# Turning a quarter of the attention blocks on VectorE and the DMA queues: a graph attention layer followed by a top-p diffusion layer

## The chip, the cores and the metric

The kernel runs on one NeuronCore of a Trainium2 chip. The core has TensorE (PE; its weight loads are listed apart as PEld), VectorE (DVE), ScalarE (ACT), GpSimd (POOL) and SyncE (SP), which here only issues DMA transfers. The metric is the device time of one launch in microseconds (us), lower being better: a median over runs, beside one execution that the hardware profiler recorded.

## The reference

The inputs are `x` (4096 rows of 256 floats) and a 0/1 adjacency matrix `adj` (4096 x 4096). Layer 0 is a graph attention layer with four heads. Layer 1 normalizes its input and then makes two steps of a diffusion with two hops each, one over the graph and one over an attention matrix that keeps, row by row, the largest probabilities until their sum reaches 0.9. The change lies in the first of these two steps.

```python
def _top_p_attention(X, W1, W2, W3):
    q = X @ W1.T @ W2.T
    k = X @ W3.T
    probs = jax.nn.softmax(q @ k.T / TAU, axis=-1)
    idx = jnp.argsort(-probs, axis=-1)
    sp = jnp.take_along_axis(probs, idx, axis=-1)
    cs = jnp.cumsum(sp, axis=-1)
    keep_sorted = cs - sp < TOP_P
    ...
    A = probs * mask
    return A / jnp.maximum(A.sum(-1, keepdims=True), 1e-12)
...
for n in range(STEPS):              # STEPS = 2
    A = _top_p_attention(Xa, W1, W2, W3)
    Xf = R @ Xf
    Xa = A @ Xa
    Z = Z + Xf @ U1[n].T + Xa @ U2[n].T
```

## The kernel before

Rows are cut into 32 blocks (`NB`) of 128. Layer 0 and the first graph hop fill the first 1068 us or so of the span. Then comes step 0 of the top-p attention (n = 0), then step 1, which is built the same way, with the second graph hop at its start.

**One block.** For block b of 128 query rows the kernel makes 128 x 4096 logits (`logits`, L758; four calls of four matmul instructions, 512 columns each), takes their exponentials into the tile `e` on ScalarE (`exponentials`, L944), and sums them under two bounds, also on ScalarE (`first_probe`, L949, four passes over half a row). GpSimd works out a better bound `c3` from these sums in a chain of small operations (`first_step`, L968, ending at L1000). VectorE then copies everything below `c3` into the tile `big` (`third_probe`, L1015), searches `big` for the threshold (`candidates`, L1018 to L1053: 18 MAX8 passes at L1033, a reduction over 18 numbers that lie 8 floats apart at L1037, MAX8 and MATCH_REPLACE on the survivors, a scan and some small operations), and sets all smaller exponentials in `e` to zero (`masked`, L1055, the long instruction at L1058, then a reciprocal at L1059).

**The product.** `attend` (L1154) multiplies the masked row block by the 4096 x 256 matrix `X`. The matrix product wants the row block turned: its columns have to lie on the partitions. So for each of eight groups g of four column blocks, `turn` (L1121) makes four TensorE transposes of 128 x 128 squares into PSUM and one ScalarE copy of the four to SBUF (`eT`, L1126), and `gather` (L1129) makes four matmuls that add up in `acc`. Each fp32 matmul of `gather` runs as two weight loads and two passes, so a group has eight instructions at L1132. `turn` runs two groups ahead of `gather`. After the eighth group come `contributed` (L1140: four more instructions at L1142) and `scaled` (L1134: a ScalarE copy and a store to `xa_d`).

**What runs beside it.** While TensorE attends to block b, it also makes the logits of block b + 3 (`AHEAD`), a call of `logits` after each of the first two turns and after the first two gathers, and ScalarE makes their exponentials and probes. GpSimd's chain for block b + 3 follows when the probes are done. Blocks 0 to 2 are searched earlier, during the first graph hop (`picks`). The last three blocks (29 to 31) have no block ahead and make no logits.

**The order.** All of this is emitted under `manual_schedule`, so each engine runs its instructions in the order of the Python calls. For each b the loop at L1450 calls `chosen_kept(b)` (L1409), then `began` for block b + 3, then `attend(b)`. On VectorE the order in `chosen_kept(b)` is: the search of block b, `third_probe` of block b + 1, `finish` of block b - 2 (L1311), `masked` of block b. Block 31 has no `third_probe` behind it. On the SP queue the order around a block is: the store to `xa_d` of block b - 1 (it waits for the end of that block's product), the store to `z_d` of `finish`, two small loads of `q_s` for a later block (L770), the load of `xf` for block b (L1111), and then the store to `xa_d` of block b.

**Buffers.** `e` has four buffers. The pool `rp` has a tag `ar` with four buffers of 128 x 1024 floats, which hold adjacency tiles in the graph hops and lie unused while step 0 attends.

Of the kernel before, what the change touches and what calls it, by code (L numbers as in the profile page):

```python
# [11 lines left out]
F32 = mybir.dt.float32  # L12
# [14 lines left out]
P = 128  # L27
# [13 lines left out]
G0 = 8  # L41
# [15 lines left out]
def gat_then_top_p_diffusion(  # L57
# [18 lines left out]
    nc = tc.nc  # L76
# [4 lines left out]
    NB = N // P  # L81
# [6 lines left out]
    dram = ctx.enter_context(tc.tile_pool(name="dram", bufs=1, space=bass.MemoryType.DRAM))  # L88
# [33 lines left out]
    rp = ctx.enter_context(tc.tile_pool(name="rp", bufs=2))  # L122
# [35 lines left out]

    uv_d = dram.tile([H, P, NB, 2, W3 + 1], BF16, name="uv_d")
    s_d = dram.tile([H, N], F32, name="s_d")  # L160
    adj_d = dram.tile([NB // G0, P, NB, G0 * P], F32R, name="adj_d")
    with tc.tile_pool(name="l0", bufs=1) as l0, tc.tile_pool(name="l0s", bufs=2) as l0s, tc.tile_pool(name="l0o", bufs=1) as l0o:
        passing = ctx.enter_context(ExitStack())
# [410 lines left out]
        with tc.manual_schedule(engines=every):  # L574
# [14 lines left out]
            for k in range(KC):  # L589
                for c in range(KC):  # L590
                    nc.tensor.matmul(pm[:, k, :], w_t[:, k, c, :], spots[:, c].rearrange("p t h -> p (t h)"),
                                     start=(c == 0), stop=(c == KC - 1))
# [15 lines left out]
            for n, (k, p) in enumerate(todo):  # L608
# [16 lines left out]
                if k % H == 2 and 2 < p < PAIRS - 3 and lifted:  # L625
                    b = lifted.pop(0)
# [128 lines left out]
    def bank():  # L755
        return ps2.tile([P, 2, 512], F32, name="mm")[:, 0, :]

    def logits(q, kT, c):  # L758

        pm = ps2.tile([P, 2, 512], F32, name="mm")  # L760
        for t, halves in enumerate(((0, 1), (1, 0))):
            for h in halves:
                nc.tensor.matmul(pm[:, h, :], q[t], kT[:, ds(h * (N // 2) + c * 512, 512)], start=(t == 0), stop=(t == 1))  # L763
        return pm
# [143 lines left out]
    def col(name, bufs=None):  # L908
        return small.tile([P, 1], F32, name=name, bufs=bufs or 4)
# [34 lines left out]
    def exponentials(r, c):  # L944

        ev = r.e.rearrange("p (h c n) -> p h c n", h=2, c=4)
        nc.scalar.activation(ev[:, :, c, :], r.pm[c], AF.Exp, bias=r.nm, accum_out=r.sums[:, c // 2, c % 2:c % 2 + 1])  # L947
# [107 lines left out]
    def masked(r):  # L1055

        kept, r.scale = col("kept"), col("scale")
        nc.vector.scalar_tensor_tensor(r.e, r.e, r.t, r.e, ALU.is_ge, ALU.mult, accum_out=kept)  # L1058
        nc.vector.reciprocal(r.scale, kept)  # L1059
# [24 lines left out]
    def untied(r, z, work):  # L1084
# [18 lines left out]
        nc.vector.scalar_tensor_tensor(r.e, ties, r.t, r.e, ALU.mult, ALU.add, accum_out=kept)  # L1103
        nc.vector.reciprocal(r.scale, kept)

    def block(t, b):
        return t[ds(b, 1)].rearrange("o p d -> (o p) d")

# [12 lines left out]
    def turn(r, g):  # L1121
        pt = ps3.tile([P, 4, P], F32, name="tp")
        for i in range(4):
            nc.tensor.transpose(pt[:, i, :], r.e[:, ts(4 * g + i, P)], ident)  # L1124
        eT = rows.tile([P, 4, P], F32, name="eT", bufs=3)
        nc.scalar.copy(eT, pt)  # L1126
        return eT

    def gather(r, eT, g, cur):  # L1129
        for i in range(4):  # L1130
            j = 4 * g + i
            nc.tensor.matmul(r.acc[:, 0, :], eT[:, i, :], cur[:, j, :], start=(j == 0), stop=(j == NB - 1))  # L1132

    def scaled(r):  # L1134
        if r.n + 1 < STEPS:
# [4 lines left out]
    def contributed(r):  # L1140
        for k in range(KC):
            nc.tensor.matmul(r.far, r.xf[:, k, :], S.u1[:, k, :], start=(k == 0), stop=(k == KC - 1))  # L1142
# [11 lines left out]
    def attend(r, cur, ahead, between={}, eT=()):  # L1154

        if ahead:
            ahead.pm = {}
        def start(c):
            if ahead:
                ahead.pm[c] = logits(ahead.q, ahead.kT, c)  # L1160
                exponentials(ahead, c)
        eT = list(eT) or [turn(r, 0)]
        start(0)
        loads(r)
        r.ri = rinv[:, r.b:r.b + 1]
        last = r.n + 1 == STEPS and r.b + 1 == NB
        if last:
            r.far = bank()[:, :D]
        eT.append(turn(r, 1))
        start(1)  # L1170
        for g in range(NB // 4):
            if g + 2 < NB // 4:
                eT.append(turn(r, g + 2))
            gather(r, eT[g], g, cur)
            if last and g == 4:
                contributed(r)
                weighed(r)
                gathered(r)
            if g < 2:
                start(2 + g)  # L1180
            elif g == 2 and ahead:
                summed(ahead)
            elif g in PROBED and ahead:
                first_probe(ahead, PROBED.index(g))
            if g in between:
                between[g]()
        if not last:
            contributed(r)
            weighed(r)
        scaled(r)  # L1190
# [193 lines left out]
    for n in range(STEPS):  # L1384
        cur = X
        G = SimpleNamespace()
        found = [table(f"found{i}") for i in range(3)]
        blocks = {}
        with tc.manual_schedule(engines=every):
            pieces = first_hop if n == 0 else hops(second)  # L1390
            filling, picking = fills(n, G, found, blocks), picks(n, found, blocks)
            done = 0 if n else NB - G0 - LOOK
            for i, _ in enumerate(pieces, 2 * done):
                if n > 0 and i % 6 == 1 and i // 6 < NB // 4:
                    g = i // 6
                    nc.sync.dma_start(cur[:, ts(g, 4), :], xa_d[ts(g, 4)].rearrange("b p d -> p b d"))
                if (n == 0 or i > 10) and i // 2 % NB != NB - 2:
                    next(filling, None)
                    if i // 2 % NB < NB - 3 or i % (2 * NB) == 2 * NB - 1:
                        next(picking, None)  # L1400
                if i == 2 * len(order) - 6:
                    first = turn(blocks[0], 0)
            weights(n)
            for _ in filling:
                next(picking, None)
            for _ in picking:
                pass

            def chosen_kept(b):  # L1409

                r = blocks[b]
                if not hasattr(r, "kept"):
                    candidates(r, found)
                if b > 2:
                    polished(blocks.pop(b - 3))
                if b + 1 < NB and not hasattr(blocks[b + 1], "thirded"):
                    third_probe(blocks[b + 1])
                if b > 1:
                    finish(blocks[b - 2])
                    finish_scale(blocks[b - 2])  # L1420
                if b + 2 < NB and not hasattr(blocks[b + 2], "stepped"):
                    first_step(blocks[b + 2])
                if 0 < b < NB - 1:
                    gathered(blocks[b - 1])
                if not hasattr(r, "kept"):
                    masked(r)
                if 1 < b < NB - 1:
                    normal(blocks[b - 2])

            R = SimpleNamespace(n=n, kT=G.kT, qT=G.qT, nm=G.nm, table=found[0])  # L1430

            def last_chosen():
                chosen_kept(NB - 1)
                R.failed, R.undone = questioned(G, found)

            def looked():
                counted(R)
                chosen(R)

            def beginning():  # L1440
                normal(blocks[NB - 3])
                gathered(blocks[NB - 2])
                finish(blocks[NB - 2])
                finish_scale(blocks[NB - 2])

            def asked():
                R.count = number(R, R.undone)

            beside = {NB - 2: {5: last_chosen}, 0: dict(zip((0, 1, 3, 5, 6), S.turned))}
            for b in range(NB - 1):  # L1450
                chosen_kept(b)
                if b + AHEAD < NB:
                    blocks[b + AHEAD] = began(n, b + AHEAD, G)
                attend(blocks[b], cur, blocks.get(b + AHEAD),
                       beside.get(b, {}), [first] if b == 0 else ())
            r = blocks[NB - 1]

            def earlier():
                polished(blocks[NB - 3])
                finish_rows(blocks[NB - 2])  # L1460

            beside = {0: beginning, 1: looked, 3: earlier, 4: asked}
            if n + 1 < STEPS:
                second = hop_of(n + 1)
                beside.update({2: lambda: (both_weights(), begin(second, 5)), 5: lambda: split(second, 2), 6: lambda: (split(second, 5), own(second, 5))})
            attend(r, cur, None, beside)
            for m in range(second.begun if n + 1 < STEPS else 0):
                for s in range(KC):
                    graph_products(second, m, s, (0,))
            finish(r)  # L1470
            finish_scale(r)
            finish_rows(r)
        repaired(R, cur)
# [32 lines left out]
```

## Time and profile before

| What | us |
|---|---|
| Median of three runs | 2820.71 (2817.5 to 2821.74) |
| The profiled execution | 2820.09 |
| Its span, first to last instruction | 2818.1 |
| Step 0, first turn to the last product's store | 1068.4 to 1768.4 |
| One block of step 0 (1404.34 to 1426.27, store to store) | 21.93 |
| TensorE's mean granted clock, as a share of full speed | 0.996 |

The profile's page gives the busy time of each engine over the span, the same in 40 equal slices (about 70 us each), the DMA queues, and the costliest groups of instructions, each with a count, a mean duration and the idle time of its engine in front of it with what ended that idle time. Other views give busy time in chosen windows, the list of waits, and instructions in order of time. Durations of neighbours on an engine overlap a little: the next instruction of VectorE can start some 0.07 us before the one in front of it is said to end, so that a sequence is best read from start to start.

### The profile page before, as it was taken

The page shows a single profiled execution, that of the slowest core. Times are in us where ns is not written, and L with a number is a line of the kernel's source. Part 1 is how long each engine was busy: PE and PEld are TensorE (multiplying, and loading weights), DVE is VectorE, ACT ScalarE, POOL GpSimd, SP SyncE. Part 2 cuts the span into 40 slices and gives each one's busy share as a digit, 9 for nine tenths or more (in the row PEclk, how much of TensorE's full clock was granted, in tenths as well). Part 3 has the DMA queues.
Part 4 walks back from the last instruction along what each step waited for, and adds up shares of the span by engine and source line. Part 5 has one row for each costly group of instructions (what it writes and reads, how often), then busy time and mean ns, then how long its engine had stood idle before and what let it go on. Part 6 is the DMA issues. An engine that isn't in the chain of part 4 may idle for free. (4 is left out here: it accounts for less than half of the span.)

```text
span 2818.1 us, 51577 instructions
## 1 busy us (share of the span) xinstructions
PE 2772.0 (98%) x18791; PEld 2443.1 (87%) x18791; DVE 2164.6 (77%) x5067; ACT 1925.4 (68%) x3066; POOL 907.2 (32%) x1895
## 2 busy tenths in 40 slices
PE   6999999999999999999999999999999999999998
PEld 5899999999988888888888888667878888888887
DVE  8877878778654385999989997333574999999997
ACT  8867886879633636888888884232627878887882
POOL 7311121111011231223332231000304666666664
PEclk9999999999999999999999999999999999999999
DMA  9969597695376782000000002667991111111110
GB/s 204 255 247 197 210 233 196 228 203 217 143 229 213 242 305 94 21 21 21 27 20 21 21 24 69 217 196 239 332 348 50 32 34 40 31 32 32 37 34 26
DMA packets 174114, 376.44 MB, mean 134 GB/s; under 512 B 18198, under 2 KB 123542, under 8 KB 169750
## 3 DMA queue, kind: packets, MB, share of 16 engines
q1 hardware_dynamic: 142496, 271.12, 29.9%
q0 software_dynamic: 26112, 97.53, 13.8%
q10 hardware_dynamic: 5238, 4.35, 0.5%
q8 instruction: 153, 2.51, 0.4%
q14 instruction: 115, 0.94, 0.1%
HBM read 305.48 MB, written 113.57 MB: 149 GB/s over the span
## 5 line engine op out<-in xcount | busy, mean ns | idle before, releaser
L1132 PE MATMUL acc<-X,eT 128*128 128x256 f32 x4096 | 948.0, 379 | 0.0
L1132 PEld LDWEIGHTS acc<-X,eT 128*128 128x128 f32 x4096 | 748.1, 190 | 85.7
L400 PE MATMUL acc<-ut,m 128*128 128x195 bf16 (+1 forms) x8192 | 698.1, 246 | 1.2 <-DVE m L379 0.9
L400 PEld LDWEIGHTS <-m 128*128 128x128 fp8e4 x8192 | 696.8, 97 | 2.4 <-DVE m L379 1.5
L372 ACT ACTIVATE g<-sr,d_big 128x1024 uint8<-128x1024 f32 x448 | 473.0, 1135 | 9.9 <-DVE m L378 9.9
L947 ACT ACTIVATE e<-mm,nm 128x1024 f32<-128x1024 f32 x256 | 286.4, 1119 | 178.3 <-PE mm L763 167.4
L1126 ACT COPY eT<-tp 128x512 f32<-128x512 f32 x512 | 297.0, 581 | 80.1 <-PE tp L1124 79.8
L1033 DVE MAX8 cand<-big 128x8 f32<-128x228 f32 (+1 forms) x1152 | 348.3, 380 | 0.0
L646 PE MATMUL mm<-ar,hl 128*128 128x512 f32 x848 | 336.4, 407 | 3.8 <-DMA ar<-adj_d 1.7
L1015 DVE SCALAR_TENSOR_TENSOR big<-e,c 128x4096 f32<-128x4096 f32 x58 | 261.4, 4506 | 87.0 <-POOL c L1000 56.9
L646 PE MATMUL acc<-ar,hl 128*128 128x512 f32 x848 | 324.1, 393 | 1.3 <-DVE ar L490 1.3
L1124 PE MATMUL tp<-ident,e 128*128 128x128 f32 x2048 | 306.4, 273 | 5.3 <-ACT eT L1126 3.1
L1124 PEld LDWEIGHTS tp<-ident,e 128*128 128x128 f32 x2048 | 254.2, 141 | 65.7 <-ACT eT L1126 4.5
L378 DVE TENSOR_TENSOR m<-g,ax 128x512 uint32<-128x512 uint32 x256 | 188.7, 737 | 97.4 <-PE acc L400 76.9
L1058 DVE SCALAR_TENSOR_TENSOR e<-e,found 128x4096 f32<-128x4096 f32 x58 | 259.0, 4466 | 0.0
L954 ACT ACTIVATE void<-e,c 128x2048 int8<-128x2048 f32 x128 | 257.0, 2008 | 0.9
L954 ACT ACTIVATE void<-e,c1x 128x2048 int8<-128x2048 f32 x128 | 256.9, 2007 | 0.9
L971 POOL TENSOR_TENSOR sums<-sums 128x2 f32<-128x2 f32 x64 | 12.7, 199 | 623.7 <-ACT void L954 622.2
L379 DVE TENSOR_TENSOR m<-m,ax 128x512 uint32<-128x512 uint32 x256 | 183.2, 715 | 25.7 <-PE acc L400 0.5
L646 PEld LDWEIGHTS mm<-ar,hl 128*128 128x128 f32 x848 | 159.6, 188 | 43.7 <-issue 9.5
L763 PE MATMUL mm<-kT,qT 128*128 128x512 f32 x512 | 192.4, 457 | 1.5 <-ACT e L947 1.5
L646 PEld LDWEIGHTS acc<-ar,hl 128*128 128x128 f32 x848 | 159.3, 188 | 37.7 <-issue 4.1
(311 smaller groups left out, 3525.6 us busy)
## 6 DMA issues: line engine op xcount, KB each, us to landing
ar<-adj_d SPq DMA_DIRECT2D x212, 512.0 KB, 4.7
adj_d<-ax POOLq DMA_DIRECT2D x32, 2048.0 KB, 7.7
ut<-uv_d SPq DMA_DIRECT2D x60, 784.0 KB, 6.4
aru<-adj_d SPq DMA_DIRECT2D x44, 512.0 KB, 4.5
ax<-in_adj_t_dram POOLq DMA_DIRECT2D x32, 512.0 KB, 18.3
x<-xf_d SPq DMA_DIRECT2D x78, 128.0 KB, 5.2
xf<-xft_d SPq DMA_DIRECT2D x64, 128.0 KB, 2.3
sr<-s_d SPq DMA_DIRECT2D x15, 512.0 KB, 4.9
```

Source lines behind the costliest of these rows:

```text
L372: nc.scalar.activation(g[:, c, :], shared[k].sr, AF.Relu, scale=BIG, bias=d_big[:, h, j:j + 1])
L400: nc.tensor.matmul(shared[k].acc[i][:, t, :cols], m[t][:, c, ts(i, P)], shared[k].ut[j // QUARTER][:, j % QUARTER, t, :cols], start=(j == ...
L646: nc.tensor.matmul(A.acc[c][s], A.hl[m][:, t, ts(s, P)], A.ar[m][:, ts(c, 512)], start=(j == 0 and t == 0), stop=(j == NB - 1 and t == 1))
L763: nc.tensor.matmul(pm[:, h, :], q[t], kT[:, ds(h * (N // 2) + c * 512, 512)], start=(t == 0), stop=(t == 1))
L947: nc.scalar.activation(ev[:, :, c, :], r.pm[c], AF.Exp, bias=r.nm, accum_out=r.sums[:, c // 2, c % 2:c % 2 + 1])
L954: nc.scalar.activation(void, r.e[:, ts(h, N // 2)], (AF.Relu, AF.Sign)[i], bias=r.c1, scale=-1.0, accum_out=r.sums[:, h, 2 + i:3 + i])
L1015: nc.vector.scalar_tensor_tensor(big, r.e, r.c3, r.e, ALU.is_le, ALU.mult, accum_out=r.low3)
L1033: nc.vector.max(cand[:, s, :], big[:, edges[s]:edges[s + 1]])
L1058: nc.vector.scalar_tensor_tensor(r.e, r.e, r.t, r.e, ALU.is_ge, ALU.mult, accum_out=kept)
L1124: nc.tensor.transpose(pt[:, i, :], r.e[:, ts(4 * g + i, P)], ident)
L1126: nc.scalar.copy(eT, pt)
L1132: nc.tensor.matmul(r.acc[:, 0, :], eT[:, i, :], cur[:, j, :], start=(j == 0), stop=(j == NB - 1))
```

## The change

For blocks 3 to 30 of step 0 the last quarter of the row block, the eight column blocks 24 to 31 (`SENT` = 24), is no longer turned by TensorE. Directly behind `masked(r)` the new function `sent(r)` is called. One VectorE instruction transposes 32 x 32 squares inside the 1024 last columns of `e` and writes them to a tile `staged`, arranged so that the eight column blocks are interleaved: neighbours in a row of a square land 8 floats apart. A square that has been turned in place lies on the wrong group of 32 partitions, so DMA moves it: four stores of 128 KB each put the squares into a DRAM tensor `turned_d` (one store for each group of 32 columns, in runs of 1 KB), and one load of 512 KB, which has to wait for the four, brings them back to a tile `landed` with each square on its right partitions, 4 KB for each partition. All five DMAs are issued from SP. In `attend`, groups 6 and 7 are not turned (no transposes, no `eT` copy), and their eight matmuls in `gather` take their weights from `landed`, where the 128 floats of one partition lie 8 floats apart. Both tiles use the `ar` buffers, two for each block. Blocks 0 to 2 and 31 of step 0 and all of step 1 are left as they were.

```diff
+    turned_d = dram.tile([NB, 4, 32, 4, 2 * P], F32, name="turned_d")
...
+    SENT = NB - 8
+
+    def sent(r):
+        wide, many = (NB - SENT) * 32, NB - SENT
+        stage = rp.tile([P, G0 * P], F32, name="staged", tag="ar", bufs=4)
+        nc.vector.transpose(stage[:, :4 * wide].rearrange("p (c s b) -> p c b s", c=4, b=many),
+                            r.e[:, ds(SENT * P, many * P)].rearrange("p (b c r) -> p c b r", b=many, c=4))
+        landed = rp.tile([P, G0 * P], F32, name="landed", tag="ar", bufs=4)
+        for c in range(4):
+            nc.sync.dma_start(turned_d[r.b, c].rearrange("r q x -> q r x"), stage[:, ts(c, wide)])
+        nc.sync.dma_start(landed[:, :4 * wide], turned_d[r.b].rearrange("c r q x -> (c r) (q x)"))
+        r.landed = landed[:, :4 * wide].rearrange("p (i b) -> p b i", b=many)
...
     def gather(r, eT, g, cur):
...
-            nc.tensor.matmul(r.acc[:, 0, :], eT[:, i, :], cur[:, j, :], start=(j == 0), stop=(j == NB - 1))
+            nc.tensor.matmul(r.acc[:, 0, :], r.landed[:, j - SENT] if eT is None else eT[:, i, :], cur[:, j, :], start=(j == 0), stop=(j == NB - 1))
...
     def attend(r, cur, ahead, between={}, eT=()):
...
-                eT.append(turn(r, g + 2))
+                eT.append(None if hasattr(r, "landed") and 4 * (g + 2) >= SENT else turn(r, g + 2))
...
     def chosen_kept(b):
...
                 if not hasattr(r, "kept"):
                     masked(r)
+                    if b < NB - 1 and r.n == 0:
+                        sent(r)
```

## The prediction

> **What bounds the kernel now.** First the page's busy times, its slices and the granted clock:
>
> ```profile
> PE 2772.0 (98%) x18791; PEld 2443.1 (87%) x18791; DVE 2164.6 (77%) x5067; ACT 1925.4 (68%) x3066; POOL 907.2 (32%) x1895
> ...
> PE   6999999999999999999999999999999999999998
> ...
> DVE  8877878778654385999989997333574999999997
> ...
> PEclk9999999999999999999999999999999999999999
> ```
>
> TensorE is busy nearly throughout at full clock. Step 0 (1068 to 1768 us) covers slices 16 to 25, where VectorE shows nines as well. So the stage has to be read for itself, in the view of busy time by windows (PE, PEld, DVE, ACT, POOL):
>
> ```profile
> 1400.00:1500.00 100.00, 100.00 (x529) 86.85 (x528) 89.72 (x239) 81.27 (x131) 35.06 (x110) 1.00 0.08 24
> ```
>
> In 100 us of step 0 TensorE has no gap, VectorE is busy 89.7 us and ScalarE 81.3. The list of waits between 1200 and 1600 us says what VectorE's rest is:
>
> ```profile
> DVE big L1015 <- POOL c L1000: 27.2, 18, 1.5
> ```
>
> Once in each of 18 blocks, 1.51 us on average, `third_probe` waits for GpSimd's `c3`. Beside the small gaps between its instructions that is all the time VectorE has off. Then the timeline of one block:
>
> ```profile
> 1412.01 4.48 DVE L1015 SCALAR_TENSOR_TENSOR big<-e,c 128x4096 f32<-128x4096 f32 x1 [1.51 <-POOL c L1000]
> ...
> 1414.75 0.60 PE L1124 MATMUL tp<-ident,e 128*128 128x128 f32 x4
> ...
> 1415.19 1.89 PE L1132 MATMUL acc<-X,eT 128*128 128x256 f32 x8
> ...
> 1416.81 4.47 DVE L1058 SCALAR_TENSOR_TENSOR e<-e,found 128x4096 f32<-128x4096 f32 x1
> 1416.92 0.60 PE L1124 MATMUL tp<-ident,e 128*128 128x128 f32 x4
> ...
> 1419.52 5.34 PE L1132 MATMUL acc<-X,eT 128*128 128x256 f32 x24
> ...
> 1421.21 0.08 DVE L1058 DVE_READ_ACCUMULATOR e<-e,found 128x1 f32 x1
> ...
> 1424.70 1.03 PE L1142 MATMUL acc<-u,xf 128*128 128x256 f32 x4
> ...
> 1425.35 0.58 PEld L1124 LDWEIGHTS tp<-ident,e 128*128 128x128 f32 x4
> ```
>
> Three things are to be seen. **A group** (four transposes, eight passes) lasts 1416.92 - 1414.75 = 2.17 us; 24 passes alone last 1424.70 - 1419.52 = 5.18 us, 0.216 each; so four transposes cost 2.17 - 8 x 0.216 = 0.44 us. **VectorE's lead**: `masked` ends at 1421.29 and TensorE first needs it at 1425.35, 4.1 us later. **The periods**: `third_probe` starts at 1149.06, 1170.98 and 1192.89, a block each 21.92 us, TensorE's pace. VectorE without its wait would need 21.92 - 1.51 = 20.41.
>
> **The change part by part.** *Removed from TensorE:* eight transposes for each of 28 blocks, 2 x 0.44 = 0.89 us a block. TensorE alone would run at 21.03, and the most that can be won is 28 x 0.89 = 24.9 us. *Removed from ScalarE:* two copies of 0.58 us; with 19% of its time free it bounds nothing, so this counts as nothing (were that idle time gone, it would be a gain of up to 1.16 us a block).
>
> *Added to VectorE:* one transpose of 128 x 1024 floats a block, behind `masked`. Nothing waits for it at once (TensorE's first turn waits for `masked` only), but the search of the next block is queued behind it, and behind that the next `masked`. VectorE's period becomes 20.41 + T, where T is counted from start to start. With T over 0.62 VectorE is slower than TensorE's 21.03 and its lead runs out; with T over 1.51 it is slower than today. No row shows this instruction. Its floor is a comparison of 1024 elements (L370) that took 720 ns at the shortest, T = 0.65. At one element a cycle, the slope of the reductions below (1.06 ns), with 0.14 us fixed and 0.07 off for the overlap, T = 1.16. Its ceiling is the slowest kind of row per element: the scan (L1045) took 326 ns for 48 elements beside 196 ns for one element (L1036), 2.8 ns each, T = 2.9. Between them stands what the instruction does that most of VectorE's rows don't: it writes neighbours 8 floats apart. One row reads at just this step, the reduction over the eighth of each eight candidates; beside it stand a reduction over 512 neighbours and one over 32 at a step of 2:
>
> ```profile
> L829 DVE TENSOR_REDUCE lengths<-xs x16: 685/686/689, 830.7 to 1914.5; 128x8 f32<-128x512 f32 x16
> ```
> ```profile
> L847 DVE TENSOR_REDUCE km<-lengths x2: 178/178/178, 903.3 to 1924.4; 128x1 f32<-128x32 f32 x2
> ```
> ```profile
> L1037 DVE TENSOR_REDUCE found<-cand x64: 174/184/191, 996.0 to 2777.1; 128x1 f32<-128x18 f32 x64
> ```
>
> The first two give (686 - 178) / 480 = 1.06 ns an element and 144 fixed, so 18 elements should take 163 ns. They took 184 (174 to 191): 1.17 ns more for each (0.6 to 1.6). At 1.06 + 1.17 = 2.23 ns, T = 1024 x 2.23 + 0.14 - 0.07 = 2.35 us; with the shortest and longest of that row, 1.79 and 2.74. I take 2.35, since this row shares engine and step; that it reads where the transpose writes, and that 21 ns are small, is why both ends are kept.
>
> [...]
>
> *The stage's end.* Blocks 29 to 31 have no logits and TensorE needs only 18.64 us for each (1710.44, 1729.08, 1747.78), so today's lead has shrunk to 1.0 at block 30 (`masked` ends at 1728.12). From `masked` of block 3 to that of block 30 are 27 periods; the change of the end is 27 x (20.41 + T - 21.92) less this 1.0, and less some 0.5 that block 30's product still saves: **27 x (T - 1.51) - 1.5**. With T = 2.35 that is 22.7 - 1.5 = +21.2 us.
>
> *Moved to PE's weight loads:* 16 loads a block from `landed`, whose floats lie 8 apart. Rows of such a load are missing; the nearest and the longest of its size:
>
> ```profile
> L1132 PEld LDWEIGHTS acc<-X,eT 128*128 128x128 f32 x4096 | 748.1, 190 | 85.7
> ...
> L591 PEld LDWEIGHTS b<-spots,w_t 128*128 128x128 f32 x8 | 1.8, 332 | 0.0
> ```
>
> A load of 190 ns hides under a pass of 216. Up to 216 the new ones cost nothing; at 332 (the longest row, at the kernel's start) each adds 0.116, 1.86 us a block, and TensorE's period is 22.89. Up to 323 they lie under VectorE's 22.76. I take nothing, because VectorE's period covers them, and keep 332 for the range: 28 x (22.89 - 21.92) = +27. [...]
>
> *Added to SP:* four stores and a load a block, behind the store to `xa_d` of the block before and ahead of the two `q_s` loads and `xf`. An issue takes up to 0.55 us (1.10 for two `q_s`).
>
> ```profile
> q_s<-qT SPq DMA_DIRECT2D x128, 32.0 KB, 1.9
> xa_d<-xa SPq DMA_DIRECT2D x32, 128.0 KB, 1.7
> ...
> X<-xa_d SPq DMA_DIRECT2D x8, 512.0 KB, 5.2
> ```
>
> Counted from `masked`: 2.35 for the squares, 4 x 0.55 to issue, 1.8 to land, 0.55 to issue the load, which waits for the four, 5.2 to land (the 512 KB row): 12.1 us. The first pass of group 6 starts 17.6 us into a block today (1403.64 to 1421.25) and 16.7 with two turns gone, so 4.6 us are spare. `q_s` serves a later block, and `xf` is needed 20 us in, so their delay of some 5 us is hidden too. DRAM and the 7% DMA share (the page's slices show 20 to 27 GB/s here) leave room for 1 MB a block.
>
> *The sum:* 2820.09 (the profiled execution, of which 2818.1 is span; 0.6 under the median of the runs) + 21.2 = **2841 us**.
>
> **The rivals.** *The transpose runs at an element a cycle.* For it: the tensor reductions and arithmetic all do; against it: the 184 ns row. T = 1.16 gives 27 x (-0.35) - 1.5 = -11: 2809 us, **faster**. It decides for T under 1.57, and clears 0.2% under 1.36. At 0.65 TensorE bounds again, at up to -24.9: 2795.
>
> *Weight loads bound.* For it: 16 loads with no adjacent floats; against it: 133 ns of room over today's load. From 323 ns on it takes VectorE's place; at 332 2847; were the loads slowed as much as that reduction's elements (2.23 / 1.06, 400 ns), TensorE's period would be 21.03 + 16 x 0.184 = 23.97 and the time 2820 + 28 x 2.05 = 2877.
>
> *The load lands too late.* It would show at group 6, and decide from 4.6 + 1.7 us of lateness on (1.7 being VectorE's excess over TensorE); with the slowest 512 KB row of the page, 18.3 us for `ax`, the load would come at 25.2, 8.5 late, and the time grow by 28 x (21.03 + 8.5 - 21.92) = 213 us. Against it: that row belongs to layer 0 under heavy traffic.
>
> *A T near the break-even*, 1.36 to 1.78: within 5.6 us of today.
>
> **How the numbers follow.** VectorE's write bounds, T from 1.79 to 2.74: 0.52, its own range 2826 to 2852. Weight loads: 0.14. Late landing: 0.04. An element a cycle or faster: 0.19. Near the break-even: 0.11. Two tenths of a percent, 5.6 us, is what a measurement can tell from no change: faster 0.19, same 0.11, slower 0.70. The range takes in half of the element-a-cycle case, 2809, and reaches on the other side into the weight loads, 2857.
>
> **What would show it.** A VectorE row of 28 transposes near 2.4 us; no more wait of `third_probe` for GpSimd; instead TensorE idle once a block, some 1.7 us, at the first turn, waiting for `masked`; a period of 22.8 us. Loads from `landed` above 216 ns with passes spaced wider in the last 16 of a block would show the second rival, a wait on `landed` at group 6 the third. A transpose near 1.2 us would make the forecast wrong.

## The result, and the profile after

The changed kernel takes **2832.64 us** (median of six runs, 2829.75 to 2836.16) against 2820.56 for the kernel before in the same session (2817.5 to 2821.74): **12.1 us slower**, a ratio of 1.0043 [1.0032, 1.0055]. The forecast was 2841, 21.2 us slower, inside a range of 2809 to 2857. Direction and mechanism held; the size was nearly twice too large. The profiled execution of after has a span of 2831.0 us, where before had 2818.1.

Line numbers from 161 on are one higher in after, and those behind the new function 14 higher (L1058 is now L1059, L1124 is L1138, L1132 is L1146). The busy times of the page come first:

```profile
PE 2764.8 (98%) x18567; PEld 2443.1 (86%) x18567; DVE 2219.0 (78%) x5095; ACT 1904.0 (67%) x3010; POOL 928.8 (33%) x1895
```

TensorE has 224 instructions fewer (28 blocks, eight transposes each), VectorE 28 more and 54.4 us more to do. Averaged over the span that changes no percentage by more than one; what it does to step 0 has to be read there. The busy time in the same 100 us as before, in the same columns (PE, PEld, DVE, ACT, POOL):

```profile
1400.00:1500.00 100.00, 96.15 (x485) 84.28 (x484) 97.69 (x220) 76.52 (x121) 39.27 (x106) 1.00 0.22 66
```

TensorE and VectorE have changed places. TensorE had no gap and now stands idle for 3.9 us of 100; VectorE rose from 89.7 to 97.7 and has nothing left but the seams between its instructions. The list of waits between 1200 and 1600 us (who waited for whom: total, times, longest) says it by name:

```profile
PEld tp L1138 <- PE acc L1156: 17.1, 15, 1.2
...
PE tp L1138 <- DVE e L1059: 11.5, 15, 0.8
```

The 18 waits of `third_probe` for GpSimd's `c`, 27.2 us before, are gone from the list. In their place TensorE waits at the first turn of a block, for the `e` that `masked` writes, 0.77 us at a time; the weight loads in front of that turn stand longer (1.14 us), since the last loads of the block before end some 0.4 us ahead of their passes. The two new kinds of instruction, with their shortest, median and longest durations in ns:

```profile
L1112 DVE STREAM_TRANSPOSE staged<-e x28: 2024/2176/2228, 1136.4 to 1739.5; 128x1024 f32<-128x1024 f32 x28
```
```profile
L1146 PEld LDWEIGHTS acc<-X,landed x448: 312/336/338, 1157.1 to 1758.8; 128*128 128x128 f32 x150
```

And the timeline of one block (start, duration, engine, line, what):

```profile
1399.39 4.47 DVE L1059 SCALAR_TENSOR_TENSOR e<-e,found 128x4096 f32<-128x4096 f32 x1
...
1404.02 0.63 PE L1138 MATMUL tp<-ident,e 128*128 128x128 f32 x4 [0.77 <-DVE e L1059]
...
1404.09 2.17 DVE L1112 STREAM_TRANSPOSE staged<-e 128x1024 f32<-128x1024 f32 x1
...
1406.10 5.37 DVE L1034 MAX8 cand<-big 128x8 f32<-128x227 f32 x18
...
1406.29 2.31 SPq L1116 DMA_DIRECT2D turned_d<-staged  x4
...
1414.33 0.33 SPq L1117 DMA_DIRECT2D landed<-turned_d  x1
...
1416.94 4.48 DVE L1016 SCALAR_TENSOR_TENSOR big<-e,c 128x4096 f32<-128x4096 f32 x1
...
1420.78 3.98 PE L1146 MATMUL acc<-X,landed 128*128 128x256 f32 x16
...
1421.74 4.48 DVE L1059 SCALAR_TENSOR_TENSOR e<-e,found 128x4096 f32<-128x4096 f32 x1
...
1424.59 1.03 PE L1156 MATMUL acc<-u,xf 128*128 128x256 f32 x4
```

Four readings. **The period**: from `masked` to `masked` 1421.74 - 1399.39 = 22.35 us (21.92 before). **The transpose** is said to last 2.17 us, yet the search behind it starts 1406.10 - 1404.09 = 2.01 us after it; over the 28 blocks this distance is 1.87 to 2.05, mean 1.98. **The passes** from `landed` are 16 in 1424.59 - 1420.78 = 3.81 us, 0.238 each instead of 0.216, although each load lasts 336 ns. **The queue**: the four stores are issued by 1408.60, but the load leaves only at 1414.33, 5.7 us later.

What a reader who stops at the period would miss lies at the end of the stage. In the rows below TensorE comes to block 30's first turn, where it has no logits to fill its time:

```profile
1735.28 1.03 PE L1156 MATMUL acc<-u,xf 128*128 128x256 f32 x4
...
1739.39 2.93 PE L1138 MATMUL tp<-ident,e 128*128 128x128 f32 x12 [3.09 <-DVE e L1059]
1742.12 3.56 PE L1146 MATMUL acc<-X,eT 128*128 128x256 f32 x8
1745.51 0.60 PE L1138 MATMUL tp<-ident,e 128*128 128x128 f32 x4
```

Eight passes take 3.56 us here, where a row of eight takes 1.89 elsewhere in step 0. The view by windows has the granted clock in the third place from the end:

```profile
1735.00:1736.40 1.40, 1.30 (x6) 0.82 (x5) 1.40 (x1) 0.06 (x1) 0.00 (x0) 1.00 0.00 0
1739.39:1745.00 5.61, 5.61 (x19) 4.79 (x20) 5.60 (x15) 1.75 (x3) 0.00 (x0) 0.50 0.12 32
```

After 3.09 us of idleness TensorE was granted half its clock for the whole 5.6 us of the second window. Its 12 transposes and first eight passes took 1745.51 - 1739.39 = 6.12 us; the same set took 1763.71 - 1760.16 = 3.55 in block 31, at a clock of 1.00. So behind the wait the same work took 2.57 us more. That sum belongs to this execution: in two of the kernels below the same set took 5.09 us after a wait of 3.92 ("The queue") and 6.14 after one of 3.57 (eight blocks, sorted), 1.5 and 2.6 us over 3.55. The waits of 0.77 us, once a block, left the clock at 1.00 in the window from 1400 to 1500 us. How long a wait must be for the clock to fall was not shown.

### The profile page after: what moved, and what is told of

Same layout as the page of the kernel before. It is cut to its first block, busy times and chain, and to the rows that moved or that the text cites. A ratio compares the mean times of both kernels' runs of the same rounds, so it can differ in the third digit from the quotient of the medians.

```text
span 2831.0 us, 51301 instructions
## 1 busy us (share of the span) xinstructions
PE 2764.8 (98%) x18567; PEld 2443.1 (86%) x18567; DVE 2219.0 (78%) x5095; ACT 1904.0 (67%) x3010; POOL 928.8 (33%) x1895
## 5 line engine op out<-in xcount | busy, mean ns | idle before, releaser
L1146 PE MATMUL acc<-X,eT 128*128 128x256 f32 x3648 | 843.7, 380 | 0.0
L1146 PEld LDWEIGHTS acc<-X,eT 128*128 128x128 f32 x3648 | 668.5, 191 | 77.5
L1140 ACT COPY eT<-tp 128x512 f32<-128x512 f32 x456 | 264.1, 580 | 98.7 <-PE tp L1138 98.7
L1138 PEld LDWEIGHTS tp<-ident,e 128*128 128x128 f32 x1824 | 225.5, 141 | 84.9 <-PE acc L1156 24.0
L1138 PE MATMUL tp<-ident,e 128*128 128x128 f32 x1824 | 274.6, 274 | 23.9 <-DVE e L1059 20.3
L1059 DVE SCALAR_TENSOR_TENSOR e<-e,found 128x4096 f32<-128x4096 f32 x58 | 259.1, 4467 | 0.0
L972 POOL TENSOR_TENSOR sums<-sums 128x2 f32<-128x2 f32 x64 | 39.2, 612 | 607.1 <-ACT void L955 607.1
```

The source lines that it names most:

```text
L1146: nc.tensor.matmul(r.acc[:, 0, :], r.landed[:, j - SENT] if eT is None else eT[:, i, :], cur[:, j, :], start=(j == 0), stop=(j == NB - 1))
```

## The experiments

The theory is the prediction's: VectorE's round bounds step 0, and it grew because the transpose writes neighbours 8 floats apart. Rivals: TensorE's loads from `landed`, 336 ns long where a pass takes 216, bound; the squares arrive late; or sending the squares is a loss whatever the layout.

Where a kernel's time can't be compared with the others' as a whole, the **stage** is used: from the start of `masked` of block 3 to the last store to `xa_d` in step 0, 636.4 us before and 648.7 after. Its difference, 12.3, is the whole of the 12.1. The two ends of the stage, in before and then in after:

```profile
1131.96 4.47 DVE L1058 SCALAR_TENSOR_TENSOR e<-e,found 128x4096 f32<-128x4096 f32 x1
...
1768.37 0.34 SPq L1138 DMA_DIRECT2D xa_d<-xa  x1
```
```profile
1131.80 4.48 DVE L1059 SCALAR_TENSOR_TENSOR e<-e,found 128x4096 f32<-128x4096 f32 x1
...
1780.47 0.36 SPq L1152 DMA_DIRECT2D xa_d<-xa  x1
```

**Two layouts, separated.** A square's write and its read share one layout: what the transpose writes in steps lies in steps for TensorE, unless something sorts it. To vary one without the other, the squares of four kernels hold zeros, so that their order is of no account. In these four and in the two kernels without squares further down, the last quarter of the product of blocks 3 to 30 in step 0 is left out. Step 1 then starts from other values and searches far longer, some 2190 us more in all of them (in the control 279 instructions of 4.48 us at L1072, which the kernel before never runs). The expectations below, which name times near 2800, did not foresee that. These kernels are compared with each other and by their stages. The first is the control:

```diff
+    blank = l1.tile([P, 32], F32, name="blank")
+    nc.gpsimd.memset(blank, 0.0)
...
         nc.vector.transpose(stage[:, :4 * wide].rearrange("p (c s b) -> p c b s", c=4, b=many),
-                            r.e[:, ds(SENT * P, many * P)].rearrange("p (b c r) -> p c b r", b=many, c=4))
+                            blank[:, None, None, :].to_broadcast([P, 4, many, 32]))
```

> The changed kernel with one thing replaced: the squares are taken from 32 zeros read again and again instead of from the exponentials, so that the last quarter of blocks 3 to 30 adds nothing to the product of step 0. All instructions, layouts and transfers stay. It is the reference for the next three. Theory W (VectorE's scattered write bounds): transposes of 2.0 to 2.2 us, a period of 22.35 us in step 0, about 2833 us. Theory L (the weight loads from landed bound) and theory D (the transfers, or their landing, cost the time) expect the same here.

The next three start from it and take one or both of these edits: the first makes VectorE write neighbours side by side, the second makes TensorE read them side by side.

```diff
-        nc.vector.transpose(stage[:, :4 * wide].rearrange("p (c s b) -> p c b s", c=4, b=many),
+        nc.vector.transpose(stage[:, :4 * wide].rearrange("p (c b s) -> p c b s", c=4, b=many),
...
-        r.landed = landed[:, :4 * wide].rearrange("p (i b) -> p b i", b=many)
+        r.landed = landed[:, :4 * wide].rearrange("p (b i) -> p b i", b=many)
```

> As e0_blank, but VectorE writes the 32 floats of a square's row side by side, and TensorE reads 128 floats side by side from landed. Transfers unchanged. Theory W: the transpose falls to about 1.2 us, 1.16 from start to start, VectorE's period to 20.35 + 1.16 = 21.5, TensorE's is 21.03; the time is 27 x (21.5 - 21.92) - 1.5 = -13 us against the kernel before, about 2808. Theory L: loads back at 190 ns, also about 2808 or less. Theory D: no change against e0_blank, 2833.

> As e0_blank, but only VectorE's write has its neighbours side by side; TensorE still reads landed at a step of 8 floats. Theory W: period 21.5 us (TensorE with its slow loads needs 21.03 + 16 x 0.022 = 21.4), about 2808 us. Theory L: loads still 336 ns, the time stays near 2833. Theory D: 2833.

> As e0_blank, but only TensorE's loads read side by side; VectorE still writes at a step of 8 floats. Theory W: period 22.35 us as in e0_blank, about 2833 us, only TensorE's wait for masked grows by some 0.36 us a block. Theory L: loads of 190 ns, the time falls to 2808 or less. Theory D: 2833.

| Kernel | Time, us | Ratio to before | Stage | Period | Transpose, ns | Load, ns |
|---|---|---|---|---|---|---|
| control | 5023.09 | 1.7825 [1.7795, 1.7855] | 647.3 | 22.36 | 2173 | 336 |
| both adjacent | 5003.07 | 1.7751 [1.7721, 1.7781] | 626.8 | 21.55 | 1245 | 190 |
| write adjacent | 5002.33 | 1.7747 [1.7718, 1.7777] | 626.6 | 21.55 | 1245 | 336 |
| read adjacent | 5024.26 | 1.7827 [1.7797, 1.7856] | 647.2 | 22.34 | 2184 | 190 |

The control has the period of after, so zeros do no harm to the question. The rows of the write-adjacent kernel, then of the read-adjacent one:

```profile
L1114 DVE STREAM_TRANSPOSE staged<-blank 128x1024 f32<-128x1024 f32 x28 | 34.8, 1244 | 0.4
...
L1148 PEld LDWEIGHTS acc<-X,landed 128*128 128x128 f32 x448 | 109.2, 335 | 1.0 <-DMA landed<-turned_d 0.3
```
```profile
L1114 DVE STREAM_TRANSPOSE staged<-blank 128x1024 f32<-128x1024 f32 x28 | 60.6, 2165 | 0.4
...
L1148 PEld LDWEIGHTS acc<-X,landed 128*128 128x128 f32 x448 | 85.0, 190 | 12.2 <-DMA landed<-turned_d 0.7
```

Each edit does what it should to its own row: 2165 to 1244 ns for the transpose, 335 to 190 for the load (count and form, then busy us and mean ns, then idle time before). Only the first moves the stage, by 20.7 us; the second moves it by no more than 0.2, alone or on top. VectorE's write is the bound, and the loads, at 335 ns or at 190, are not.

**TensorE alone.** What does taking the turns away bring if the squares cost nothing? Here no squares are made or sent, and the weights of the last eight column blocks are one tile of zeros, read side by side; a second kernel reads them 8 floats apart.

```diff
-        nc.vector.transpose(stage[:, :4 * wide].rearrange("p (c s b) -> p c b s", c=4, b=many),
...
-        r.landed = landed[:, :4 * wide].rearrange("p (i b) -> p b i", b=many)
+        if not hasattr(S, "blank"):
+            S.blank = rp.tile([P, G0 * P], F32, name="blank", tag="ar", bufs=4)
+            nc.gpsimd.memset(S.blank, 0.0)
+        r.landed = S.blank.rearrange("p (b i) -> p b i", b=NB - SENT)
```

In the second kernel the last line has the pattern of after, "p (i b) -> p b i".

> The changed kernel without transposes and transfers: the weights of groups 6 and 7 of blocks 3 to 30 are read from one tile of zeros, 128 floats side by side, so that this quarter adds nothing to the product. It shows what TensorE alone can win: 28 x 0.89 = -25 us, about 2796, period 21.03.

> As e5_no_squares, but the zeros are read at a step of 8 floats. It prices the loads by themselves: 336 ns each but only 0.022 us a pass, period 21.4, about 2806 us. Theory L, in its strong form (each load's 336 ns over the 216 of a pass is paid in full, 1.9 us a block): period 22.9, about 2847.

The first took 4989.49 us (1.7696 [1.7669, 1.7723]) with a stage of 611.7 and a period of 21.03; the second 4995.83 (1.7721 [1.7694, 1.7748]), 621.6 and 21.38. The stage is 24.7 us shorter than before: the most that there was to win. The loads' price can be read where VectorE isn't in the way, in TensorE's timeline of the second kernel:

```profile
1434.14 3.98 PE L1141 MATMUL acc<-X,blank 128*128 128x256 f32 x16
1437.96 1.03 PE L1151 MATMUL acc<-u,xf 128*128 128x256 f32 x4
```

Sixteen passes in 3.82 us; side by side they take 1435.63 - 1432.17 = 3.46. A load that lasts 146 ns longer delays its pass by 0.36 / 16 = 0.022 us. Consecutive loads overlap each other: in after, 16 of them, 336 ns each, are done in 3.89 us and not in 5.4. The whole price is 0.35 us a block, and with VectorE at 22.35 it is hidden.

**Both engines loaded.** In this kernel the squares are made and sent as in after, but nobody uses them: TensorE turns all eight groups itself.

```diff
-        r.landed = landed[:, :4 * wide].rearrange("p (i b) -> p b i", b=many)
+        r.unused = landed[:, :4 * wide].rearrange("p (i b) -> p b i", b=many)
```

> The changed kernel with TensorE turning all 32 column blocks as before; squares and transfers are made but nobody reads them. The result is complete. Theory W: VectorE's period is 22.35 us as in the changed kernel, so that giving TensorE its eight transposes back costs next to nothing: about 2833 us. Theory L: without loads from landed the time goes back to 2821. Theory D, if landing late is the cost: 2821, since nobody waits for landed.

It took 2833.15 us (1.0045 [1.003, 1.0061]), stage 647.9: TensorE's 0.89 us a block given back changes nothing. Its wait for `masked` only shrinks, from 15 waits with 11.5 us in the same stretch to these:

```profile
PE tp L1138 <- DVE e L1059: 2.1, 8, 0.3
```

So all of TensorE's saving in after goes into waiting for VectorE, but for the 0.35 us a block that its slower loads take.

**Half the squares.** Four column blocks in place of eight are sent, so the step is 4 floats and half as much is written.

```diff
-    turned_d = dram.tile([NB, 4, 32, 4, 2 * P], F32, name="turned_d")
+    turned_d = dram.tile([NB, 4, 32, 4, P], F32, name="turned_d")
...
-    SENT = NB - 8
+    SENT = NB - 4
```

> The changed kernel with SENT = NB - 4: only the last four column blocks go by squares and DMA (512 floats a partition, neighbours 4 floats apart). Theory W: half the transpose, about 1.0 us from start to start, VectorE's period 20.35 + 1.0 = 21.35; TensorE saves 0.44 and pays 8 x 0.022 for its loads, 21.65; so TensorE bounds again and the time is 28 x (21.65 - 21.92) = -8 us, about 2813. Theory D, if the cost comes with every transfer: still slower than the kernel before, 2826 or more.

2811.86 us (0.9974 [0.9963, 0.9984]), faster than before by 7.5: stage 627.5, period 21.62 (TensorE's 21.65 was expected). The transpose, with its count and durations:

```profile
L1112 DVE STREAM_TRANSPOSE staged<-e x28: 1104/1126/1147, 1135.5 to 1719.2; 128x512 f32<-128x512 f32 x28
```

1.13 us lies under the 1.51 that VectorE had to spare, and the kernel gains. With this layout the change was a loss by its size: the same idea below the break-even pays.

**The queue.** Only the cut of the four stores changes: by groups of 32 partitions instead of groups of 32 columns, so that the outermost dimension of a store is 32 and not 4.

```diff
-        for c in range(4):
-            nc.sync.dma_start(turned_d[r.b, c].rearrange("r q x -> q r x"), stage[:, ts(c, wide)])
+        for q in range(4):
+            nc.sync.dma_start(turned_d[r.b, :, :, q].rearrange("c r x -> r c x"),
+                              stage[ts(q, 32), :4 * wide].rearrange("r (c x) -> r c x", c=4))
```

> The changed kernel with its four stores cut by groups of 32 partitions instead of by groups of 32 columns, so that the outermost size of each is 32 and not 4; bytes and runs stay. If only 4 of the 16 DMA engines carried a store before (the DMA share of 0.2 during the stores), the load is issued some 3 us earlier after the stores. Theory W: the time stays at 2833 us, since landed was in time already but for the last two blocks. Theory D: it falls.

It took 2833.4 us (1.0051 [1.0036, 1.0067]). SP's rows in one block:

```profile
1407.12 1.77 SPq L1116 DMA_DIRECT2D turned_d<-staged  x4
1410.92 0.34 SPq L1118 DMA_DIRECT2D landed<-turned_d  x1
```

The load leaves 3.80 us after the first store; in after it was 8.04. The time does not move, so lateness of the squares isn't what cost the 12 us. The DMA share while the stores ran (second place from the end), first in after, then here:

```profile
1407.00:1414.00 7.00, 7.00 (x39) 6.08 (x38) 6.79 (x28) 4.42 (x8) 4.49 (x13) 1.00 0.24 75
```
```profile
1408.00:1411.00 3.00, 3.00 (x17) 2.57 (x16) 3.00 (x11) 1.85 (x5) 2.45 (x8) 1.00 0.68 172
```

The share is the mean over 16 engines: 0.24 is 3.8 engines' worth, at 75 GB/s, against 0.68, 10.9, and 172. The two kernels differ in the cut of the stores alone; what ties the share to the outermost size, 4 or 32, was not shown.

**The squares written side by side, complete.** TensorE is to read the 128 weights of a column block as one run; a tile written in runs of 32 has them in four places, so it has to be sorted first. The load can do that, in four parts with runs of 128 bytes:

```diff
-        nc.vector.transpose(stage[:, :4 * wide].rearrange("p (c s b) -> p c b s", c=4, b=many),
+        nc.vector.transpose(stage[:, :4 * wide].rearrange("p (c b s) -> p c b s", c=4, b=many),
...
-        for c in range(4):
-            nc.sync.dma_start(turned_d[r.b, c].rearrange("r q x -> q r x"), stage[:, ts(c, wide)])
-        nc.sync.dma_start(landed[:, :4 * wide], turned_d[r.b].rearrange("c r q x -> (c r) (q x)"))
-        r.landed = landed[:, :4 * wide].rearrange("p (i b) -> p b i", b=many)
+        for q in range(4):
+            nc.sync.dma_start(turned_d[r.b, :, :, q].rearrange("c r x -> r c x"),
+                              stage[ts(q, 32), :4 * wide].rearrange("r (c x) -> r c x", c=4))
+        for q in range(4):
+            nc.sync.dma_start(landed[:, :4 * wide].rearrange("p (b q s) -> p q b s", b=many, q=4)[:, q],
+                              turned_d[r.b, :, :, q].rearrange("c r (b s) -> (c r) b s", b=many))
+        r.landed = landed[:, :4 * wide].rearrange("p (b i) -> p b i", b=many)
```

Two more kernels take this with six and with four column blocks (`SENT = NB - 6` and `NB - 4`, `turned_d` cut to fit); with six, `turn` makes two transposes instead of four in group 6:

```diff
-                eT.append(None if hasattr(r, "landed") and 4 * (g + 2) >= SENT else turn(r, g + 2))
+                n = min(4, SENT - 4 * (g + 2)) if hasattr(r, "landed") else 4
+                eT.append(turn(r, g + 2, n) if n > 0 else None)
```

> A complete kernel with both sides adjacent: VectorE writes the rows of its squares side by side, TensorE's weights lie side by side, and DMA does the sorting between them, with four stores of one partition group each (1 KB runs) and four loads whose runs are 128 bytes. Theory W: transposes of 1.25 us, period 21.55 us as in e1_both_adjacent, 27 x (21.55 - 21.92) - 1.5 = -11 us, about 2808 us, if the short runs land before group 6. Theory D: the short runs land late, TensorE waits for landed at group 6 in every block, and the time is above 2820.

> As e8_load_sorts, with six column blocks instead of eight; group 6 makes two transposes, group 7 none. Theory W: transpose 1.25 - 256 x 1.04 ns = 0.98 us, VectorE's period 21.55 - 0.27 = 21.28, TensorE's 21.92 - 6 x 0.111 = 21.25: the two meet, and the time is 27 x (21.28 - 21.92) - 1.5 = -19 us, about 2801.

> As e8_load_sorts, with four column blocks. Theory W: VectorE's period 21.0, TensorE's 21.92 - 0.44 = 21.48; TensorE bounds: 28 x (21.48 - 21.92) = -12 us, about 2807; some 4 less than e4_four_blocks, which pays for its loads at a step of 4.

| Blocks sent | Time, us | Ratio to before | Stage | Period | Transpose, ns |
|---|---|---|---|---|---|
| eight | 2809.59 | 0.9969 [0.9957, 0.9981] | 627.2 | 21.54 | 1245 |
| six | **2804.00** | 0.9946 [0.9933, 0.996] | 618.4 | 21.27 | 978 |
| four | 2806.58 | 0.996 [0.9946, 0.9974] | 623.7 | 21.49 | 711 |

The edit of the write that brought 20.7 us with zeros brings 21.4 here together with the sort in the load, and nothing is left out (a stage of 627.2 against after's 648.7). All three beat both kernels, and no pass waits for `landed` in any of them. Six were expected 19 us faster than before: the medians show 14.7 and the stage 18.0. Their windows from 1400 to 1500 us, for eight, six and four:

```profile
1400.00:1500.00 100.00, 98.72 (x503) 84.88 (x502) 97.21 (x234) 80.71 (x126) 32.00 (x97) 1.00 0.34 69
```
```profile
1400.00:1500.00 100.00, 100.00 (x517) 86.83 (x516) 97.23 (x228) 82.11 (x132) 30.88 (x98) 1.00 0.27 57
```
```profile
1400.00:1500.00 100.00, 100.00 (x524) 86.87 (x523) 95.47 (x231) 82.17 (x133) 32.95 (x104) 1.00 0.22 49
```

With eight TensorE still has gaps and VectorE is full; with four VectorE has room again; with six both are full, and that is the fastest. Of the 8.8 us between the stages of eight and six, 6.5 lie in the 27 periods. The rest lies behind them: with eight, TensorE waits 3.57 us at block 30's first turn, and its first 12 transposes and eight passes then take 6.14 us, as in after; with six it waits 0.57, and the same set takes 1715.35 - 1711.77 = 3.58. The periods fit the two engines' own rounds: TensorE 21.92 - 0.11 a transpose taken away, that is 21.48 for four, 21.26 for six and 21.03 for eight; VectorE 20.35 (worked out below) and the transpose less its overlap with the next instruction. The longer of the two is the period.

## Why the prediction was right in kind and too large

**The mechanism was right**: VectorE becomes the bound, `third_probe` no longer waits for GpSimd from block to block, TensorE waits once a block for `masked`, and the period is longer than before. Each of these is in the trace, and the layout kernels show that it is the write.

**T, the transpose from start to start, was mis-sized**: 2.35 us taken, 1.98 measured. Its parts, from the instruction's length at two sizes side by side (1245 ns for 1024 floats, 711 for 512: 1.04 ns each and 0.18 fixed): in steps of 8 a float costs (2176 - 177) / 1024 = 1.95 ns, not 2.23, which is 0.29 us; the fixed part is 0.18 instead of 0.14; and the successor starts some 0.17 us before the end, not 0.07 (0.08 where the write is side by side). The 2.23 came from 21 ns in a reduction that *reads* at that step. That row pointed to the kind of cost, and its ends (1.79 to 2.74) held the value. But it priced a write by a read, an analogy that no run here tests, and 18 elements were too few to size it. The rival's "element a cycle" is the slope of rows: 1.06 ns in the reductions, and 1.04 in f32 arithmetic (693 ns for 512 elements at L828, 192 for 32 at L871). No run shows VectorE's cycle, and not all arithmetic has that slope: L370 took 720 ns for 1024 elements, 0.70 each with all that is fixed.

**VectorE's sum**: `masked` of block 3 to `masked` of block 30 took 591.7 us before and 603.0 after, so 27 periods grew by 11.3, 0.42 each. The prediction's rule gives 27 x (1.98 - 1.51) = 12.7; the rest of VectorE's round turned out 0.05 us shorter than the 20.41 taken (22.33 - 1.98 = 20.35), and that is the difference.

**The stage's end, -1.5, had the wrong sign**: it was +1.0. The lead of block 30 went as predicted (0.8 us against 1.0), and block 31 brought 0.3. But block 30's product, which was to save 0.5, took 20.77 us instead of 18.70: the 2.57 us of half clock after the wait of 3.09. The prediction counted the end of the stage in time alone and did not ask what the granted clock would do after a long wait. 11.3 + 1.0 = 12.3. The +1.0 is the least certain term: with the stores cut by partitions ("The queue") VectorE's round is the same, the clock was low for less of the work (0.50 from 1741.3 to 1743.0 and 0.75 on the mean from there to 1746.0, the set done in 5.09 us), and from `masked` of block 30 to the last store it took 44.7 us, as in before, instead of after's 45.7.

**TensorE's largest gain**, 24.9 us and a period of 21.03, was confirmed at 24.7 and 21.03. None of it reached the end, as the kernel with unused squares shows.

**Wait at the first turn**: "some 1.7 us a block" was 0.77 by the row, since 22.35 and not 22.8 is the period and since the loads from `landed` fill 0.35 of the difference. 22.35 - 21.03 - 0.35 = 0.97, of which 0.2 is not accounted for.

**Weight loads**: costing them at nothing was right, but the reason was not. The prediction set a load's duration, 332 ns, against a pass of 216 and so had a rival that would bind from 323 on. The loads did last 336, and cost 0.022 each, not 0.120. The rival had a chance of 0.14 by a rule against which the prediction's own row of L591 speaks: eight loads of 332 ns would fill 2.66 us one after another, and that row has them busy for 1.8, so they overlap there too.

**Spare time of the squares**: 4.6 us predicted, some 2 found. The DMA share falls from 0.52 to 0.04 at 1418.6, 14.7 us after `masked` ended (12.1 predicted), and group 6 starts 16.9 after it. The stores took 5.7 us to land behind the last issue where 1.8 was taken from a store of the same size. Without logits to cover it the load is late at the end of the stage: 0.48 us at 1731.25.

## What to carry to other kernels

When work moves from the bounding engine to one that is nearly as busy, set both engines' rounds side by side and move only as much as makes them equal: a quarter moved lost 12 us, the same quarter written side by side won 9, and three quarters of it 15. A layout that suits the reader can cost the writer more than the work that was moved: here 0.93 us a block (2176 ns against 1245), where the turns were worth 0.89. So price the write by a row that writes in that step (a read at that step gave 2.23 ns a float, the write took 1.95), and let a transfer that is needed anyway do the sorting (eight blocks, sorted, landed with no pass waiting). Price a weight load by the spacing of its passes, not by its duration (146 ns longer, 0.022 us a pass), and price an idle TensorE by its wait and by the clock that follows (3.09 us, and 2.57 more at half clock).

## What the runs showed unexpectedly

**Loads overlap.** Weight loads that read 8 floats apart last 336 ns instead of 190, yet their passes follow at 0.239 us instead of 0.216 ("TensorE alone").

**A GpSimd instruction stretched sevenfold.** In the same stretch of step 0, `sums` took 197 ns before and this in after:

```profile
L972 POOL TENSOR_TENSOR sums<-sums x18: 194/1444/1473, 1204.2 to 1581.4; 128x2 f32<-128x2 f32 x18
```

It now starts while VectorE's `masked` runs (1402.48 for 1.44 us, beside `masked` from 1399.39) and ends with it. Near the stage's start, where it ran behind the end of `masked` (at 1140.15 and 1161.40, with `masked` over at 1136.28 and 1158.41), it took 0.20. That `masked` is the cause was not tested. No instruction of VectorE waits for GpSimd between 1200 and 1600 us any more, so it costs nothing here.

**The transpose is slower in the middle of the stage.** It takes 2.02 to 2.05 us where GpSimd is idle beside it (the first three blocks, and the last) and mostly 2.15 to 2.23 where GpSimd's chain runs. But block 29, where GpSimd is busy beside it for 1.6 us, has 2.06 and makes no logits, so GpSimd need not be the cause. Why was not tried.
